# Moving a rare-case branch behind the last store, and reordering the first layer's chunks

## The chip, the core and the metric

The kernel runs on one core of a Trainium2 chip. The metric is device time in microseconds, as the median of several runs. A core has five engines that work side by side, each on its own list of instructions in order: TensorE (PE in the profile, its weight loads PEld), VectorE (DVE), ScalarE (ACT), GpSimd (POOL) and SyncE (SP). They wait for one another by semaphores. SP issues nearly all transfers from the chip's memory.

## The reference, cut to what matters

Four graph layers over 3327 nodes with 64 features and a dense, mostly zero adjacency matrix `adj` (3327 x 3327). After each layer the input is added and each row is normalised.

```python
def _L0_gnn_ref(features, adj, W):
    neigh = jnp.matmul(adj, features)
    deg = jnp.sum(adj, axis=1, keepdims=True) + 1.0
    return jnp.matmul(jnp.concatenate([features, neigh / deg], -1), W.T)

def _L1_gnn_ref(x, adj, weight, bias):      # hyperbolic log map of every pair of nodes
    w = adj / jnp.maximum(adj.sum(axis=1, keepdims=True), 1e-08)
    log_ij = _logmap(x[:, None, :], x[None, :, :], c)
    agg = jnp.einsum('ij,ijc->ic', w, log_ij)
    return _expmap(jnp.zeros_like(agg), agg @ weight + bias, c)

def _L2_gnn_ref(X, adj, W, b):              # mean over neighbours, relu, row norm
    ...

def _L3_gnn_ref(input, adj, weight, bias):
    support = input @ weight
    mask = (adj != 0).astype(support.dtype)
    rank = jnp.cumsum(mask, axis=1)         # which neighbour in the row is it?
    deg = rank[:, -1:]
    k = jnp.minimum(deg, float(MAX_NEIGH))
    pos = rank - (deg - k)
    w = mask * jnp.where(pos > 0, DECAY ** (k - pos), 0.0)
    return w @ support + bias

x = _layernorm(x + _L0_gnn_ref(x, adj, L0_gnn_W), axis=-1)
x = _layernorm(x + _L1_gnn_ref(x, adj, L1_gnn_weight, L1_gnn_bias), axis=-1)
x = _layernorm(x + _L2_gnn_ref(x, adj, L2_gnn_W, L2_gnn_b), axis=-1)
x = _layernorm(x + _L3_gnn_ref(x, adj, L3_gnn_weight, L3_gnn_bias), axis=-1)
```

## The kernel before

**Tiling.** The nodes are padded to 3328, that is 26 blocks of 128. The transposed adjacency is cut into four chunks of 832 target nodes (columns), and each chunk into 13 pairs of source blocks. One pair is a tile of 128 x 2 x 832 floats, 832 KB; `load_adj` brings it, by SP, into one of four rotating buffers (`adjp`) or into memory that is free for a while, such as `sums` or `uw`. Each layer reads the whole matrix again, chunk by chunk.

**Layer 0.** For each pair, `aggregate_pair` (L467) adds adjacency times features to the accumulator of the chunk in PSUM: 4 instructions, 8 records in the trace. The loop also does early work for layer 3, which needs every neighbour's rank. For three of the four chunks (all but `LATE_RANKS`, chunk 3) `Ranks.mask` makes a 0/1 mask of the pair on VectorE (L493). `count` turns masks into ranks: 12 matmuls of the mask with a triangle of ones (L539), a carry of the last row into the next mask on VectorE (`carry`, L525), and two copies to `rank` on ScalarE (L549). Masks that are made wait in a list, and `count(masked, places, left, ...)` works it down until `left` of them remain. Before, the chunks come in the order 0, 3, 1, 2 (`ORDER`), so the unranked chunk 3 stands second; the counts of chunk 0 are spread over chunks 0 and 3 (`L0_SPILL`), and in chunks 1 and 2 three masks stay behind (`L0_LAG`). They are counted after the last adjacency matmul.

Each chunk completes the sums of a group of blocks (`GROUPS`). `finish0` takes the group through `sums0` (transposes L582, division by the degree L590, sum of squares) and `features0` (the scaled features `xr` and `xu`, partly on GpSimd), in steps that are laid between the pairs of the next chunk. `transposes0` (L650) then writes the group into `ut` and `wt`, the two operands of layer 1. The last group goes through `sums0` at the end of the layer, and through `features0` and its transposes in layer 1's loop (`late`).

**The vote and the branch.** Layer 1 is computed for pairs of nodes. If all nodes have a large enough norm, a cubic in the scalar product is precise enough, which is `layer1_far`, the cubic path. If one has not, the general arm `layer1_near` must run. `sums0` notes the near nodes (L594) of each group; at the end of layer 0 VectorE, TensorE and VectorE reduce them to one number `n_near` (L775, L777, L778). Every engine loads it (L1466) and branches (L1468). For these inputs it is zero. Both arms go on with `layers_2_and_3`.

**Layer 1, cubic path.** For each of 104 items (chunk, source block) `far_v` (L835) multiplies `wt` and `ut` into one of three PSUM banks, VectorE forms the product p with the adjacency (L846), ScalarE squares (L859, L860, or L851), GpSimd or VectorE finishes the factor s (L861, L854), and `far_aggregate` (L866) adds it to the chunk's sum six items later. The first two pairs are loaded into `sums`, once the layer 0 sums there have been read; the loads of the others come after the branch.

**Order.** The instructions of each engine are placed by a scheduler; `issue_after` forces an instruction behind another on its engine, and is used all over to write the order down.

Of the kernel before, what the change touches and what calls it, by code (L numbers as in the profile page):

```python
# [41 lines left out]

ORDER2 = (2, 3, 1, 0)
# [35 lines left out]
L0_SPILL = 6  # L79
# [39 lines left out]
def four_gnn_layers_kernel(  # L119
# [148 lines left out]
    xu = nodes.tile([P, NB, D + 2], FP, name="xu")  # L268

# [305 lines left out]
    def sums0(c, bank):  # L575


        b0, b1_, nb = blocks_of(c)
        last = c == ORDER[-1]
# [25 lines left out]
    def features0(c, y, ss, work, aside=False):  # L605


        b0, b1_, nb = blocks_of(c)
# [31 lines left out]
    def finish0(c, bank):  # L640
        y, ss = yield from sums0(c, bank)
        yield from features0(c, y, ss, Work(blocks_of(c)[2]), True)

    def transposes0(c, place, behind=None, aside=False, k0=0, k1=GB):

        b0, _, nb = blocks_of(c)
# [11 lines left out]

    with ExitStack() as l0s:
        banks = Banks(l0s, "l0psum")  # L660
# [61 lines left out]
        first = GROUPS[3][0] * P  # L722
        load_xt(slice(first, NP))
        loaded = {jp: load_adj(ORDER[0], jp) for jp in (12, 11, 10)}
        load_xt(slice(0, first))
        masked, issued, counted, side = [], None, None, None
        for n, c in enumerate(ORDER):
# [4 lines left out]
            for jp in reversed(range(NB // 2)):  # L732
# [11 lines left out]
                left = (L0_SPILL - jp // 2 if ranks else jp // 2) if n < 2 else L0_LAG  # L744
# [3 lines left out]
                if side is not None and jp < NB // 2 - 1:  # L748
                    on_array = jp == NB // 2 - 2
                    if not step(side, (counted or issued) if on_array else mask if ranks else None):  # L750
                        side = None
                        transposes0(ORDER[n - 1], places.free(), counted or issued, True)
                        if n == NCH - 1:

                            nc.scalar.activation(nothing, wt[:, GROUPS[ORDER[n - 1]][0] * P].unsqueeze(1), AF.Tanh)
# [17 lines left out]
        count(masked, places, 0, counted)  # L773
        nearest = small.tile([P, 1], FP, name="nearest", tag="nearest")
        nc.vector.tensor_reduce(nearest, near, axis=AX.X, op=ALU.add)  # L775
        vote = banks.one(NCH % 2)
        nc.tensor.matmul(vote[0:1, 0:1], lhsT=nearest, rhs=ones, start=True, stop=True)  # L777
        nc.vector.tensor_copy(n_near, vote[0:1, 0:1])  # L778

    def adj_pairs(there):

        for c in ORDER:
            for jp in PAIRS:
                yield c, jp, there.pop(0) if there else load_adj(c, jp)
# [25 lines left out]
    def layer1_far(banks):  # L822
        with tc.tile_pool(name="l1w", bufs=1) as wp:
# [107 lines left out]
            work = Work(blocks_of(ORDER[-1])[2], banks.one(1))  # L931
            late = features0(ORDER[-1], *last_group, work)
            del work
            pairs = adj_pairs(first_pairs)
            waiting, last, side, total, summed, kept = [], None, None, NCH * NB, None, {}
            for start in range(0, total + L1_AHEAD, L1_GROUP):
                group = range(start, start + L1_GROUP)
                made = []
                for i in group:
                    if i < total:  # L940
# [5 lines left out]
                        v, v_issued = far_v(c, jb, summed)  # L946
# [3 lines left out]
                for i in group:  # L950
# [18 lines left out]

                    if late is None and i in (late_at, late_at + 2):  # L970
                        k0, k1 = (0, 4) if i == late_at else (4, GB)
                        transposes0(ORDER[-1], banks.one(1), v_issued, False, k0, k1)
# [23 lines left out]
            own = banks.pair()[:, 0, :]  # L996
# [6 lines left out]
    def layer1_near():  # L1003
        with ExitStack() as stack:
            all_of(features0(ORDER[-1], *last_group, Work(blocks_of(ORDER[-1])[2])))
            transposes0(ORDER[-1], Banks(stack, "l1b").pair())
# [184 lines left out]
    def begin2(banks, loading, loaded, behind):  # L1191
# [3 lines left out]
        rows = last_rows([(c, rank[:, c]) for c in ORDER2 if c != LATE_RANKS])  # L1195
        next(rows)
# [6 lines left out]
    def layers_2_and_3(banks, acc, done, rows, there):  # L1203


        with tc.tile_pool(name="l2m", bufs=10) as mp, tc.tile_pool(name="late", bufs=1) as late:
# [191 lines left out]
            for n, c in enumerate(ORDER2):  # L1398
# [9 lines left out]
                for i, jp in enumerate(order):  # L1408
# [17 lines left out]
                    if i == OWN2_AT:  # L1426
                        x2, based = prologue2(c, issued)
                        if n == 0:
                            step(rows, based)
                            all_of(rows)  # L1430
# [34 lines left out]

    some_near = nc.values_load(n_near[0:1, 0:1], min_val=0, max_val=NP)  # L1466

    with tc.If(some_near == 0) as cmp:  # L1468
        with ExitStack() as arm:
            banks = Banks(arm, "psum_far")  # L1470
            layers_2_and_3(banks, *layer1_far(banks))
    with cmp.Else():
        done = layer1_near()
        with ExitStack() as arm:
            banks = Banks(arm, "psum_near")
            with tc.tile_pool(name="l2a_near", bufs=8) as more:
                loading = load_ahead2(lambda k: more.tile([P, CH], FP, name="ahead", tag="ahead"))
                acc, rows = begin2(banks, loading, next(loading), None)
# [44 lines left out]
```

## Time and profile before

| | us |
|---|---|
| median of 3 runs | 524.47 |
| lowest and highest run | 524.07, 525.8 |
| span of the profiled execution, first to last instruction | 521.7 |
| layer 0, to the end of its last adjacency matmul | 143.25 |
| first matmul of layer 1 | 153.89 |
| first matmul of layer 2 | 350.4 |

The profile is one execution, and its span is the only time that is known of it; start and end of the program around the span, and the spread of the runs, make the rest of the median. The stretches of layers are read from the timeline. In the profile's rows a group of instructions has its line, engine, operation, output and inputs by name, shapes, and how often it comes; for DMA the bandwidth and the mean busy share of 16 engines are given, and for TensorE the clock that it was granted, as a share of full speed.

### The profile page before, as it was taken

To read this page: it belongs to the slowest core of one execution; us is meant where nothing else is said; L and a number is where in the kernel's file an instruction comes from. 1 tells how busy PE (TensorE), PEld (TensorE's weight loads), DVE (VectorE), ACT (ScalarE), POOL (GpSimd) and SP (SyncE) were. 2 spreads that over 40 slices of the span, in tenths; PEclk is the share of its full clock that TensorE was granted. 3 is DMA by queue.
4 is the path that set the end of the run, shared out by engine and by line. 5 is a ranking of instruction groups with operands and counts; after the bars stand their busy time and mean duration, and the time that the engine had idled before them with its cause. 6 is when DMAs were issued, how large, how long until landed. Compare 5 with 4: busy or idle time off the path is not lost.

```text
span 521.7 us, 8496 instructions
## 1 busy us (share of the span) xinstructions
PE 482.3 (92%) x3256; PEld 240.5 (46%) x3256; DVE 387.0 (74%) x703; ACT 336.7 (65%) x395; POOL 180.1 (35%) x150
## 2 busy tenths in 40 slices
PE   4999999999977999998999999999999999999994
PEld 3554344454432333443353344354465565556663
DVE  3565438989668987789879977988789876627744
ACT  1435545776868899978988896930277943337941
POOL 2001201112026778866886785700412012200000
PEclk9999999999978999999999999999999999999997
DMA  8999999989439688767776777579869979950002
GB/s 268 318 366 339 375 389 387 327 285 315 183 99 323 203 260 291 232 196 257 260 231 213 224 256 261 197 268 405 315 197 361 306 263 374 349 194 2 1 18 56
DMA packets 46211, 132.52 MB, mean 254 GB/s; under 512 B 6966, under 2 KB 7070, under 8 KB 46098
## 3 DMA queue, kind: packets, MB, share of 16 engines
q1 hardware_dynamic: 45634, 131.35, 72.7%
q0 software_dynamic: 384, 0.52, 0.3%
q8 instruction: 27, 0.44, 0.3%
q14 instruction: 22, 0.18, 0.1%
q10 hardware_dynamic: 144, 0.03, 0.0%
HBM read 130.86 MB, written 0.85 MB: 252 GB/s over the span
## 4 chain that ended last, share of the span: by engine, by line
PE 53%; DVE 24%; ACT 10%; DMA 6%; issue 3%; POOL 0%; ACTq 0%; DVEq 0%
PE one L467 16%; PE two L1333 10%; DVE p L846 8%; PE two L835 7%; DMA adj<-in_adjt_dram 6%; PE one L866 6%; PE two L539 5%; DVE mask L525 4%; PE two L467 4%; ACT s L859 3%; DVE s L854 3%; DVE mask L493 3%; ACT s L860 2%; ACT rank L549 2%; PE two L1238 1%
## 5 line engine op out<-in xcount | busy, mean ns | idle before, releaser
L861 POOL TENSOR_TENSOR s<-s,p 128x832 f32<-128x832 f32 x67 | 130.1, 1957 | 45.6 <-ACT s L860 32.3
L846 DVE SCALAR_TENSOR_TENSOR p<-two,adj 128x832 f32<-128x832 f32 x100 | 101.0, 1018 | 19.1 <-issue 14.4
L835 PE MATMUL two<-uw 64*128 64x416 f32 x416 | 91.6, 556 | 13.3 <-DVE s L854 7.2
L549 ACT ACTIVATE rank<-two,last_bias 128x832 uint8<-128x832 f32 x78 | 71.8, 952 | 45.0 <-PE two L539 23.0
L866 PE MATMUL one<-s,xu 128*64 128x416 f32 x416 | 85.2, 524 | 0.0
L467 PE MATMUL one<-adj,x0w 128*64 128x416 f32 x416 | 82.3, 522 | 2.7 <-ACT x0w L677 1.4
L859 ACT ACTIVATE s<-two,far_bias 128x832 f32<-128x832 f32 x67 | 63.6, 950 | 23.9 <-DVE p L846 21.6
L525 DVE SCALAR_TENSOR_TENSOR mask<-two,minus_last,mask 32x832 bf16<-32x832 f32 x48 | 52.5, 1093 | 29.5 <-PE two L539 26.0
L835 PEld LDWEIGHTS two<-uw 64*128 64x128 f32 x416 | 38.3, 192 | 66.7 <-PE one L866 22.6
L1333 PE MATMUL two<-bits,parts 128*64 128x416 bf16 x624 | 62.3, 339 | 0.0
L539 PE MATMUL two<-mask,tri 128*64 128x416 bf16 x416 | 52.9, 344 | 9.3 <-DVE mask L525 6.1
L493 DVE TENSOR_SCALAR mask<-adj 128x1664 bf16<-128x1664 f32 x48 | 51.5, 1073 | 13.4 <-DMA adj<-in_adjt_dram 12.6
L860 ACT ACTIVATE s<-s 128x832 f32<-128x832 f32 x67 | 60.1, 897 | 1.9
L467 PE MATMUL one<-adj,xr 128*64 128x416 f32 x264 | 57.0, 514 | 0.0
L1333 PEld LDWEIGHTS <-parts 128*64 128x64 bf16 x624 | 36.8, 110 | 24.2 <-issue 7.3
L866 PEld LDWEIGHTS one<-s,xu 128*64 128x64 f32 x416 | 25.9, 136 | 47.5 <-issue 46.6
L467 PEld LDWEIGHTS one<-adj,x0w 128*64 128x64 f32 x416 | 29.2, 138 | 35.0 <-issue 23.8
L539 PEld LDWEIGHTS <-tri 128*64 128x64 bf16 x416 | 25.6, 110 | 41.4 <-issue 23.6
L1303 ACT ACTIVATE bits<-rank 128x1664 uint16<-128x1664 uint8 x22 | 33.6, 1579 | 15.5 <-PE two L1333 14.6
L854 DVE SCALAR_TENSOR_TENSOR s<-two,p 128x832 f32<-128x832 f32 x37 | 37.6, 1016 | 2.9 <-ACT two L851 2.5
L851 ACT ACTIVATE two<-two,far_bias 128x832 f32<-128x832 f32 x37 | 34.0, 918 | 5.1 <-DVE p L846 4.9
L549 ACT ACTIVATE uw<-two,last_bias 128x832 uint8<-128x832 f32 x26 | 24.2, 950 | 12.5 <-DVE mask L525 6.4
(270 smaller groups left out, 471.1 us busy)
## 6 DMA issues: line engine op xcount, KB each, us to landing
adj<-in_adjt_dram SPq DMA_DIRECT2D x135, 832.0 KB, 5.4
uw<-in_adjt_dram SPq DMA_DIRECT2D x7, 832.0 KB, 7.4
a<-in_adjt_dram SPq DMA_DIRECT2D x8, 416.0 KB, 6.2
sums<-in_adjt_dram SPq DMA_DIRECT2D x2, 832.0 KB, 5.9
p<-in_adjt_dram SPq DMA_DIRECT2D x4, 416.0 KB, 4.7
s<-in_adjt_dram SPq DMA_DIRECT2D x4, 416.0 KB, 6.3
uw<-in_xt_dram SPq DMA_DIRECT2D x1, 640.0 KB, 11.1
out_dram<-o SPq DMA_DIRECT2D x3, 192.0 KB, 2.5
```

The lines of the kernel that those rows point to most:

```text
L467: issued = nc.tensor.matmul(acc[h * D : (h + 1) * D, 0:HC], lhsT=x[:, 2 * jp + k, 0:D], rhs=a[:, bass.ts(h, HC)], start=(first and k == 1) ...
L493: issued = nc.vector.tensor_scalar(mask, a2, 0.0, None, op0=ALU.not_equal)
L525: ranks.carried = nc.vector.scalar_tensor_tensor(halves(last), ranks.after[P - 32 : P, :, 0:HC], minus_last[P - 32 : P, :], halves(last), ...
L539: issued = nc.tensor.matmul(counts[k][rows, h, 0:HC], lhsT=lhsT[:, rows], rhs=mask[:, of, bass.ts(h, HC)], start=lhsT is tri, stop=(k == 1 ...
L549: ranks.made = nc.scalar.activation(halves(ranks.rank[:, 2 * jp + k, :]), counts[k][:, :, 0:HC], AF.Relu, bias=last_bias,)
L835: issued = nc.tensor.matmul(v[:, h, 0:HC], lhsT=wt[rows, bass.ts(jb, P)], rhs=ut[rows, bass.ds(c * CH + h * HC, HC)], start=True, stop=True,)
L846: issued = nc.vector.scalar_tensor_tensor(halves(p), v, 0.25 - 0.5 * FD, halves(a), op0=ALU.add, op1=ALU.mult)
L859: nc.scalar.activation(halves(s), v, AF.Square, bias=far_bias, scale=-2.0)
L860: nc.scalar.activation(s, s, AF.Copy, bias=FG)
L861: nc.gpsimd.tensor_mul(s, s, p)
L866: issued = nc.tensor.matmul(acc[h * D : (h + 1) * D, 0:HC], lhsT=xu[:, jb, 0:D], rhs=s[:, bass.ts(h, HC)], start=first, stop=last,)
L1333: issued = nc.tensor.matmul(acc3[c][h * D : (h + 1) * D, 0:HC], lhsT=parts[:, 2 * jp + b, bass.ts(part, D)], rhs=bits[:, b, bass.ts(h, HC) ...
```

## The change

It has three parts, which belong together.

1. **The branch goes to the end.** The cubic path is no longer an arm: it always runs, through all layers and the stores of the output. The vote's sum and matmul move from the end of layer 0 to the end of layer 1's loop (`vote`). After the last store every engine loads `n_near` and branches. If a node was near, the general arm computes layers 1 to 3 again and stores over the output. For that, layer 0's features `xr`, which layer 1 overwrites, are copied to memory (`kept_x1`, by GpSimd's queue) when the last group is done, and read back in the arm.
2. **One set of PSUM banks** (`psum_far`) serves layer 0 and all that follows. The scheduler can now mix the end of layer 0 with the start of layer 1: `ahead_of` holds layer 1's first products behind the last counts.
3. **Layer 0 in the order 0, 1, 2, 3** (`ORDER0`, `GROUPS0`), so that the unranked chunk comes last. The number of masks that may stay behind grows from 0 to 7 over the three ranked chunks and is worked down to 0 in chunk 3 (`L0_SPILL` is 8 now, which also adds two mask buffers). The last group is blocks 19 to 25; layer 1 takes the first chunk's pairs in natural order, so that these come last.

```diff
+ORDER0 = (0, 1, 2, 3)
+GROUPS0 = {0: (0, 6), 1: (6, 13), 2: (13, 19), 3: (19, 26)}
...
-L0_SPILL = 6
+L0_SPILL = 8
...
+    kept = ctx.enter_context(tc.tile_pool(name="kept", bufs=1, space=bass.MemoryType.DRAM))
+    kept_x1 = kept.tile([P, NB, D], FP, name="kept_x1")
...
+    far = ExitStack()
+    banks = Banks(far, "psum_far")
     with ExitStack() as l0s:
-        banks = Banks(l0s, "l0psum")
...
-        for n, c in enumerate(ORDER):
+        for n, c in enumerate(ORDER0):
...
-                left = (L0_SPILL - jp // 2 if ranks else jp // 2) if n < 2 else L0_LAG
+                done = n * (NB // 2) + NB // 2 - 1 - jp
+                left = L0_SPILL * jp // (NB // 2)
+                if ranks:
+                    left = min(done // 2, L0_LAG + (L0_SPILL - L0_LAG) * done // (3 * NB // 2))
                 counted = count(masked, places, left, issued)
...
-        count(masked, places, 0, counted)
+        counted = count(masked, places, 0, counted) or counted
+
+    def vote(bank, behind):
         nearest = small.tile([P, 1], FP, name="nearest", tag="nearest")
         nc.vector.tensor_reduce(nearest, near, axis=AX.X, op=ALU.add)
-        vote = banks.one(NCH % 2)
-        nc.tensor.matmul(vote[0:1, 0:1], lhsT=nearest, rhs=ones, start=True, stop=True)
-        nc.vector.tensor_copy(n_near, vote[0:1, 0:1])
+        issue_after(nc.tensor.matmul(bank, lhsT=nearest, rhs=ones, start=True, stop=True), behind)
+        nc.vector.tensor_copy(n_near, bank)
...
-            pairs = adj_pairs(first_pairs)
+            ahead_of = counted
+            pairs = adj_pairs(first_pairs, range(NB // 2))
...
-                        v, v_issued = far_v(c, jb, summed)
+                        v, v_issued = far_v(c, jb, summed or ahead_of)
...
+                    if late is None and i == late_at:
+                        nc.gpsimd.dma_start(out=kept_x1, in_=xr)
...
-            own = banks.pair()[:, 0, :]
+            own = banks.pair()
+            vote(own[0:1, 1, 0:1], summed)
+            own = own[:, 0, :]
...
     def layer1_near():
-        with ExitStack() as stack:
-            all_of(features0(ORDER[-1], *last_group, Work(blocks_of(ORDER[-1])[2])))
-            transposes0(ORDER[-1], Banks(stack, "l1b").pair())
+        nc.sync.dma_start(out=xr, in_=kept_x1)
...
+    with far:
+        layers_2_and_3(banks, *layer1_far(banks))
+
     some_near = nc.values_load(n_near[0:1, 0:1], min_val=0, max_val=NP)
 
-    with tc.If(some_near == 0) as cmp:
-        with ExitStack() as arm:
-            banks = Banks(arm, "psum_far")
-            layers_2_and_3(banks, *layer1_far(banks))
-    with cmp.Else():
+    with tc.If(some_near > 0):
         done = layer1_near()
         with ExitStack() as arm:
             banks = Banks(arm, "psum_near")
```

Elsewhere in layer 0, `ORDER` and `GROUPS` become `ORDER0` and `GROUPS0`. `begin2` leaves out, in the general arm, the last rows of the ranks, which are there by then. By the order of instructions, the small loads of `last_rows` on GpSimd's queue move from the branch up into layer 0.

## The prediction

> **What bounds the kernel now.** I read the page's busy line first, then the busy time in eight stretches cut at the chunks of layer 0 and at the layer borders, then the timeline round the branch, and last the queue entries at the program's end. Chunk borders are the first adjacency matmuls (L467) of each chunk, found by counting eight records to a pair of blocks.
>
> ```profile
> span 521.7 us, 8496 instructions
> PE 482.3 (92%) x3256; PEld 240.5 (46%) x3256; DVE 387.0 (74%) x703; ACT 336.7 (65%) x395; POOL 180.1 (35%) x150
> ...
> core 0: us, PE busy (x) PEld busy (x) DVE busy (x) ACT busy (x) POOL busy (x), PEclk, DMA share, GB/s
> 8.70:43.40 34.70, 32.24 (x223) 17.18 (x224) 23.03 (x42) 13.52 (x18) 0.64 (x4) 1.00 0.97 331
> 43.40:73.20 29.80, 28.18 (x204) 13.20 (x202) 11.31 (x29) 17.48 (x21) 3.60 (x5) 1.00 1.00 374
> 73.20:106.20 33.00, 31.14 (x230) 14.04 (x228) 27.42 (x46) 18.72 (x24) 4.80 (x4) 1.00 0.98 357
> 106.20:143.20 37.00, 34.66 (x276) 17.89 (x274) 30.72 (x46) 28.39 (x35) 5.19 (x4) 1.00 0.76 260
> 143.20:153.90 10.70, 6.83 (x61) 3.37 (x55) 7.47 (x18) 8.60 (x11) 0.30 (x1) 0.86 0.25 82
> 153.90:172.00 18.10, 14.83 (x56) 5.91 (x56) 13.82 (x28) 11.97 (x14) 13.28 (x12) 0.80 0.88 300
> 172.00:341.00 169.00, 160.18 (x827) 66.36 (x827) 144.87 (x227) 146.16 (x173) 127.13 (x66) 1.00 0.71 233
> 341.00:522.00 181.00, 171.48 (x1388) 99.90 (x1386) 125.88 (x259) 90.33 (x101) 21.75 (x20) 0.98 0.64 224
> ```
>
> TensorE sets the pace (over 92% busy) everywhere except in the fifth and sixth stretch, the 29 us round the branch, where nothing does: 6.83 of 10.70 us, 14.83 of 18.10, and DMA at a quarter. So an edit is worth there what it takes off the chain, and elsewhere what it takes off or puts on TensorE. The second stretch is chunk 3, the unranked one, second in the old order: DMA share 1.00, so transfers help to hold it.
>
> The timeline shows the chain at the branch:
>
> ```profile
> 141.66 1.59 PE L467 MATMUL one<-adj,x0w 128*64 128x416 f32 x8
> ...
> 147.42 1.09 DVE L525 SCALAR_TENSOR_TENSOR mask<-two,minus_last,mask 32x832 bf16<-32x832 f32 x1
> ...
> 152.74 0.15 DVE L778 CAST n_near<-one 1x1 int32<-1x1 f32 x1 [1.40 <-PE one L777]
> 153.89 5.06 PE L835 MATMUL two<-uw 64*128 64x416 f32 x16 [1.18 <-ACT rank L549]
> 155.85 1.02 DVE L846 SCALAR_TENSOR_TENSOR p<-two,sums 128x832 f32<-128x832 f32 x1 [2.96 <-PE two L835]
> ```
>
> Layer 0's last adjacency matmul ends at 143.25. Only then come the last four counts (12 matmuls of 1.05 us each, with a DVE carry of 1.09 us between one and the next), the last group's sums, the vote (L777, L778), 1.0 us of register load and branch, and the first layer 1 product at 153.89. The chain of waits agrees: from 143.25 on it runs through L525, L590, L591, L409, L414, L525 and three L549.
>
> **The change, part by part.** E is the end of layer 0's last adjacency matmul, 143.25 before.
>
> 1. Chunk order and counts. Before, 35 of the 39 counts lay ahead of E, after it all 39. In the old order the records of the count's first matmuls (L539 with tri, eight to a count) give 7 counts in the first stretch (56 records), 6 in the second (48), about 9 in the third (73 in the trace), 13 in the fourth up to E. The two ranked chunks of 13 pairs that run after each other thus took 33.0 us with about 9 counts and 37.0 with 13: 1.0 us more a count, which is the 1.05 of the row. That is my ruler. The new rule for what is left over (4 after chunk 0, 6 after chunk 1, 7 after chunk 2) gives 9, 11, 12 and 7 counts:
> chunk 0: 34.7 + 2 x 1.05 = 36.8;
> chunk 1: 33.0 + 2 x 1.05 = 35.1; chunk 2: 37.0 - 1.05 = 35.9;
> chunk 3: 29.8 + 1.05 = 30.8 if the transfers still hold it, 18.2 of L467 (13 x 1.40) + 7 x 1.05 + 1.5 of sums and transposes = 27.1 if TensorE alone does. It now comes after three chunks slower than the transfers, with all four buffers full, but one more 832 KB load (the first of layer 1, into `sums`) goes into its queue; I take 28.8.
> E = 8.7 + 36.8 + 35.1 + 35.9 + 28.8 = 145.3, 2 us later than before; between 142 (deferral also shortens the waits in chunks 1 and 2) and 148.
>
> 2. The junction. After E there are no counts, no vote and no branch ahead of layer 1. What DVE still has ahead of the first product p is the old chain up to L591, 143.25 to 147.39 (the one carry in it, at 144.34, ran beside the transposes, so its going saves nothing): p(0) starts at E + 4.15. In the changed kernel's order DVE then does p(0), L409, p(1), L414, the two near steps, p(2): 1.02 + 0.62 + 1.02 + 0.61 + 0.35 = 3.6, so p(2) at E + 7.8 = 153.1. Before, p(2) started at 158.10 (the second of three products merged at 157.08). Gain 5.0. From p(2) on the same rotation of three PSUM banks and the same instructions follow, so I carry 5.0 through to the end of layer 1.
> Transfers: before, four pairs were issued at once at 153.94 and landed after 4.3 to 11.5 us. In the new SP queue three of them stand ahead of layer 0's end, waiting only for buffers. The second load into `sums` waits for the last transposes, goes out at E + 2.2 and, at the 4.5 us of the same load before, lands at E + 6.7, before p(2). At the 7.3 us that the first one took, p(2) loses 1.7: kept for the range.
>
> 3. A rule against a row. The granted clock in stretches of 2 us:
>
> ```profile
> 152.00:154.00 2.00, 0.82 (x8) 0.23 (x4) 0.15 (x1) 1.73 (x2) 0.40 (x1) 0.50 0.00 0
> ...
> 162.00:164.00 2.00, 2.00 (x8) 1.04 (x6) 0.28 (x1) 1.39 (x2) 2.00 (x2) 0.50 1.02 311
> ```
>
> TensorE starts layer 1 at half clock and falls back to it at 162. The Trainium skill, TensorE: Matmul & The Clock Gate, section "Part 1: The HAM clock gate", says that the clock halves after an idle window of about 3.4 us. After the change the first gap is shorter (products 0 to 2 end near E + 3.3, product 3 can start at E + 6.2), so by the rule the clock stays up: 16 matmuls at 0.21 instead of 0.32 us, another 1.7 us gained. The row speaks for less: the drop at 162 followed a gap of only 1.83 us (158.94 to 160.77). I take 0 and keep 1.7 for the range.
>
> 4. POOL and SP queues. The memset and three `last_a` loads move up into layer 0; the three `last_more` copies of finished ranks are spread over it. One issue is 0.51 to 0.69 us (L563, L564). Each waits for ScalarE's last rank of its chunk, and POOL's xr or xu step and the copy to `twice`, which TensorE's transposes need, stand behind it. The leftover counts are done by about the seventh pair of the next chunk, the transposes come after the eleventh, so four pairs (10 us) cover it; without the cover TensorE would lose about a pair, 2.5 us. New is the copy of xr to DRAM, 832 KB, issued by POOL after the late group. No store of that size is in the trace; by L563 its issue is 0.5 to 0.7 us, and I double the upper end to 1.4. POOL runs about 3 us ahead of its user there (a product that started on POOL at 176.22 is needed near 181), so 0; 1.4 if not. Its 2 us of transfer lie in a layer with DMA share 0.71.
>
> 5. The vote goes to the end of layer 1, where TensorE runs without a gap: 0.2 us (L777, 0.19). Load of `n_near` on SP: 0.5 us (0.475 before) between layer 2 loads that are far ahead: 0.
>
> 6. The end. Every engine now loads `n_near` and branches after its last work.
>
> ```profile
> L1468 DVEq COMPARE_BRANCH  x1: 51/51/51, 517.6 to 517.6; - x1
> L1519 DVEq DRAIN  x2: 10/45/80, 520.8 to 521.2; - x2
> ```
>
> DVE's last branch, at 517.6, is followed by nothing for 3.2 us, beside the last store (landing 2.4 to 3.0). With the load ahead of it (0.544 on DVE) DVE arrives 0.5 later, just as the store ends: +0.5. The rule that speaks against this change is in the Trainium skill, Runtime: NRT & Kernel Launch, section "Instruction fetch mechanics": a taken branch to a target outside the fetched window stalls for a fetch. The changed program has two in sequence, over the general arm and then out of the empty other arm. The old end already pays one fetch; by the row the second target lies next to the first and costs its 0.05, by the rule at worst another 3.2. I take 0.5, up to 3.7.
>
> Below nothing for parts 4 to 6: a gain is excluded for 5 and 6, which only add instructions; in 4 the six issues leave POOL's junction, but its first product waited for ScalarE there (2.44 us idle), so no gain.
>
> Sum: -5.0 + 0.2 + 0.5 = -4.3 us on the profiled span of 521.7, to 517.4. The median of the runs, 524.47, is 2.8 above the span, and nothing in that difference is touched: 520.2.
>
> **The rivals.**
> A, a larger gain (0.18). Counts held back longer let masks and carries run without holding TensorE: half of the idle in chunks 1 and 2 goes (TensorE unbusy 1.9 and 2.3 us there, and more hidden in matmuls recorded at 1.6 instead of 1.4), E near 142, the clock stays up. -5.0 - 3.3 - 1.7 + 0.7 = -9.3: 515.2. For it: TensorE waits for L525 1.0 us at 125.97. Against: a carry waits for the count before it, however many are held.
> B, slower (0.15). Three ranked chunks in a row make the chain count, carry, count the bound, since DVE has mask 1.03 and carry 1.09 for each pair and group steps between. With a pair at p us in chunks 1 and 2, E = 8.7 + 36.8 + 26p + 29.8. The gain of 150.3 - E less the 0.7 is gone at p = 2.86; the fourth stretch ran at 37.0/13 = 2.85, the third at 2.54. At 3.0, E is 153.3 and the sum +3.7: 528.2. It is slower by more than can be told from 2.92 on. For it: the old pace with a full load of counts is at the edge. Against: 11 and 12 counts, not 13.
> C, it doesn't shorten the end (0.07): the second fetch is paid in full, -4.3 + 3.2 = -1.1: 523.4. For it: five engines show 2.4 to 3.5 us after their last branch. Against: the target is adjacent.
>
> **How the numbers follow.** The likeliest case (0.60) is 520.2; its own range, E between 142.5 and 147.5 with 1.7 either way for clock and landing, is 517 to 523.2, and about 0.05 of it lies within 0.3% (1.6 us, about what a measurement of this kernel can tell from no change). Faster 0.55 + 0.18 = 0.73; same 0.05 + 0.07 = 0.12; slower 0.15. For eight in ten the range goes from 513.5 (0.05 below) to 526 (0.12 above).
>
> **What would show it.** Right: E at 145, the first p about 4 us after E and no L777 between; p(2) near 153; layer 1's first product of the last chunk and everything to the last store shifted by one amount, about 5 us; DVE's last queue entry later after its last instruction by 0.5. Wrong: E beyond 149 with L539 waiting for L525 in chunks 1 and 2 (B); a gap above 4 us between the last store's issue and the end (C); transposes waiting for POOL in chunk 1 or 2 (part 4); p(2) waiting for the load into `sums`.

## The result: slower, by 1.6%

| | before | after | forecast |
|---|---|---|---|
| median of 4 runs each, us | 524.27 | 532.43 | 520.2 |
| lowest and highest run | 522.83, 525.8 | 530.0, 533.76 | range 513.5 to 526 |
| span of the profiled execution | 521.7 | 531.7 | 517.4 |
| E, end of layer 0's last adjacency matmul | 143.25 | 153.53 | 145.3 |
| E to product p of item 20 of layer 1 | 47.58 | 41.51 | 40.5 |
| start of layer 1's last sum to start of layer 2's first matmul | 3.85 | 6.57 | 4.05 |
| first to last adjacency matmul of layer 2 | 119.61 | 121.14 | 119.61 |
| last store's issue to the end | 3.68 | 5.23 | 4.2 |

The ratio of the runs is 1.0157, with a 95% interval of 1.0119 to 1.0194. The profiled execution of the changed kernel (533.74 us) is one of its longer ones, so the spans differ by 10.0 us where the medians differ by 8.2. Everything that the table leaves out, nearly all of layer 1 and of layers 2 and 3, runs as before.

The page of the changed kernel, and its busy time in stretches cut as before the change (here and in the prediction's table a chunk ends with its last adjacency matmul, to within 0.2 us): the four chunks of layer 0, the handover to layer 1 in two pieces, layer 1, the handover to layer 2, the rest, the end. After the stretch come its length, then the busy time of PE, PEld, DVE, ACT and POOL with instruction counts, the granted clock, the DMA share and GB/s.

```profile
span 531.7 us, 8503 instructions
...
PE 486.4 (91%) x3256; PEld 243.5 (46%) x3256; DVE 385.9 (73%) x703; ACT 337.0 (63%) x395; POOL 177.9 (33%) x151
...
8.90:49.40 40.50, 36.37 (x247) 19.20 (x248) 26.21 (x45) 16.09 (x21) 1.58 (x5) 0.96 0.92 292
49.40:84.50 35.10, 32.52 (x250) 15.58 (x247) 28.29 (x46) 24.70 (x30) 4.43 (x5) 1.00 0.92 314
84.50:122.80 38.30, 33.98 (x266) 17.11 (x265) 27.93 (x45) 25.06 (x31) 4.42 (x5) 1.00 0.94 330
122.80:153.50 30.70, 29.72 (x217) 14.23 (x213) 11.87 (x29) 20.32 (x25) 3.89 (x5) 1.00 0.98 349
153.50:162.50 9.00, 5.76 (x23) 2.49 (x21) 7.39 (x16) 3.29 (x5) 2.03 (x2) 0.81 0.71 259
162.50:176.10 13.60, 10.26 (x40) 3.81 (x40) 10.97 (x27) 9.37 (x11) 7.75 (x4) 0.75 0.37 124
176.10:345.10 169.00, 160.18 (x827) 66.28 (x827) 144.73 (x227) 146.17 (x173) 127.76 (x67) 1.00 0.72 238
345.10:361.00 15.90, 15.02 (x77) 8.47 (x76) 10.73 (x25) 3.33 (x5) 0.00 (x0) 0.79 0.89 323
```

In the long stretch of layer 1, a window of 169 us as before, TensorE has the same 827 records and the same 160.18 us as before, and from product p of item 20 to the last sum it takes 155.67 us (before: 155.69): nothing is wrong there. The loss lies in four places. The first chunk takes 40.5 us, with a clock of 0.96. The third takes 38.3 and the last 30.7, with transfers at a share of 0.98 in the last. The handover from layer 1 to layer 2 ran at a clock of 0.79; before, TensorE went through it at full clock. And the end is 1.55 us longer. The handover to layer 1 is shorter, as it was meant to be.

The start of layer 0, from the timeline:

```profile
4.96 1.68 POOL L570 DMA_DIRECT2D last_a<-in_adjt_dram  x3
...
13.56 1.03 DVE L500 TENSOR_SCALAR mask<-adj 128x1664 bf16<-128x1664 f32 x1 [3.88 <-DMA adj<-in_adjt_dram]
14.50 0.61 DVE L686 COPY xr<-two 128x126 f32<-128x126 f32 x2
14.84 0.89 PE L546 MATMUL two<-mask,tri 128*64 128x416 bf16 x8 [2.87 <-DVE xr L686]
```

The third mask in the kernel before, and the transfers of the changed one between 8 and 10 us (queue: packets, MB, share of 16 engines):

```profile
11.21 1.03 DVE L493 TENSOR_SCALAR mask<-adj 128x1664 bf16<-128x1664 f32 x1 [1.64 <-DMA adj<-in_adjt_dram]
```
```profile
q1 hardware_dynamic: 175, 0.57, 80.3%
q0 software_dynamic: 47, 0.15, 22.0%
```

GpSimd issues its three last_a loads at 5 us. They run on a queue of their own, q0, beside the adjacency on q1, and the mask of the third adjacency pair can only start at 13.56 (before: 11.21). VectorE makes xr after it, TensorE needs that bank for its first count and waits 2.87 us; from 15.8 to 19.2 it then runs at half clock.

The handover to layer 1:

```profile
157.43 1.02 DVE L848 SCALAR_TENSOR_TENSOR p<-two,sums 128x832 f32<-128x832 f32 x1
...
159.48 1.76 PE L837 MATMUL two<-uw 64*128 64x416 f32 x4 [1.98 <-ACT s L861]
...
160.44 1.94 POOL L863 TENSOR_TENSOR s<-s,p 128x832 f32<-128x832 f32 x1 [6.84 <-DVE ss_last L421]
160.45 1.94 DVE L601 SCALAR_TENSOR_TENSOR near_nodes<-ss_last,real 128x7 f32<-128x7 f32 x1
162.43 0.18 DVE L790 TENSOR_REDUCE nearest<-near_nodes 128x1 f32<-128x26 f32 x1
162.53 1.95 DVE L848 SCALAR_TENSOR_TENSOR p<-two,sums 128x832 f32<-128x832 f32 x2
```

The near step of the last group in the kernel before (shortest, median and longest ns, first and last start):

```profile
L594 DVE SCALAR_TENSOR_TENSOR near_nodes<-ss_last,real x1: 166/166/166, 151.0 to 151.0; 128x7 f32<-128x7 f32 x1
```

p(0) starts at E + 3.9 and p(2) at E + 9.0. TensorE's first gap lasts 1.98 us; 1.6 us into it, at 159.1, the clock falls to half and stays there for 10.2 us. Look at the near step on VectorE: 128 x 7 elements took 1.94 us, as long as GpSimd's product that started 0.01 us before it. The same instruction took 0.17 us in the kernel before, where GpSimd was idle.

The handover to layer 2:

```profile
351.15 0.19 PE L791 MATMUL two<-ones,nearest 128*1 128x1 f32 x2
...
352.04 0.13 DVE L792 CAST n_near<-two 1x1 int32<-1x1 f32 x1
...
352.23 1.95 PE L891 MATMUL two<-w1r,uw 64*128 64x64 f32 x14 [0.89 <-DVE n_near L792]
354.10 3.25 PE L905 MATMUL two<-wl,sums 128*128 128x66 f32 x14
...
357.28 5.99 PE L474 MATMUL two<-uw,xr 128*64 128x416 f32 x24
```

The same three groups in the kernel before:

```profile
346.96 1.77 PE L889 MATMUL two<-w1r,uw 64*128 64x64 f32 x14
...
348.66 1.78 PE L903 MATMUL two<-wl,sums 128*128 128x66 f32 x14
...
350.37 4.41 PE L467 MATMUL two<-uw,xr 128*64 128x416 f32 x24
```

The vote's matmul is done at 351.34. The next one, L891, writes to the other bank of the pair that the vote is in, one tile for the program, and waits 0.89 us until VectorE has copied the vote out, which had two other instructions ahead of it. 14 matmuls of L905 then take 3.25 us (before: 1.78), as the clock fell to half at 353.7 and stayed there for 6.8 us.

The end, by the queue entries of SyncE and VectorE (how often, shortest, median and longest ns, first and last start):

```profile
L1478 SPq EVENT_SEMAPHORE  x8: 17/17/17, 527.4 to 530.0; - x8
...
L1478 DVEq COMPARE_BRANCH  x1: 72/72/72, 526.6 to 526.6; - x1
...
L1478 DVEq EVENT_SEMAPHORE  x1: 21/21/21, 529.9 to 529.9; - x1
```
```profile
L1525 SPq EVENT_SEMAPHORE  x14: 17/28/28, 530.1 to 531.6; - x14
```

The last store, before and after (KB, us from issue to landing):

```profile
out_dram<-o SPq DMA_DIRECT2D x1, 128.0 KB, 2.6
```
```profile
out_dram<-o SPq DMA_DIRECT2D x1, 128.0 KB, 3.4
```

The 1.55 us have two parts. The last store, issued at 526.47, landed at 529.91, after 3.44 us, where it took 2.62 before: 0.82. From there to the end it is 1.79 us, before 1.06: 0.73. SyncE waits for the last store inside the branch (L1478), until 530.0. Only then comes the program's own closing row of waits (L1525), the first twelve of which took from 530.1 to 530.8. In the kernel before, nine of those twelve waits were over while the store was still under way.

### The profile page after: what moved, and what is told of

It reads as the page before. It is cut to its first block, busy times and chain, and to the rows that moved or that the text cites. A ratio compares the mean times of both kernels' runs of the same rounds, so it can differ in the third digit from the quotient of the medians.

```text
span 531.7 us, 8503 instructions
## 1 busy us (share of the span) xinstructions
PE 486.4 (91%) x3256; PEld 243.5 (46%) x3256; DVE 385.9 (73%) x703; ACT 337.0 (63%) x395; POOL 177.9 (33%) x151
## 4 chain that ended last, share of the span: by engine, by line
PE 52%; DVE 22%; DMA 10%; ACT 8%; issue 3%; POOL 1%; ACTq 0%; POOLq 0%; DVEq 0%
PE one L474 17%; DMA adj<-in_adjt_dram 10%; PE two L1340 10%; DVE p L848 8%; PE two L546 6%; PE two L837 5%; PE one L868 4%; DVE s L856 4%; PE two L474 4%; ACT s L861 3%; ACT s L862 3%; DVE mask L532 2%; DVE mask L500 2%; PE two L905 1%; PE two L1245 1%
## 5 line engine op out<-in xcount | busy, mean ns | idle before, releaser
L837 PE MATMUL two<-uw 64*128 64x416 f32 x416 | 93.9, 553 | 15.4 <-ACT s L861 7.7
L474 PE MATMUL one<-adj,x0w 128*64 128x416 f32 x416 | 83.8, 531 | 1.6 <-DMA adj<-in_adjt_dram 1.0
L500 DVE TENSOR_SCALAR mask<-adj 128x1664 bf16<-128x1664 f32 x48 | 50.4, 1051 | 23.0 <-DMA adj<-in_adjt_dram 22.5
L546 PE MATMUL two<-mask,tri 128*64 128x416 bf16 x416 | 52.5, 342 | 11.3 <-DVE mask L532 6.6
L474 PE MATMUL one<-adj,xr 128*64 128x416 f32 x264 | 58.1, 514 | 0.2 <-DMA adj<-in_adjt_dram 0.2
```

The lines of the kernel that those rows point to most:

```text
L474: issued = nc.tensor.matmul(acc[h * D : (h + 1) * D, 0:HC], lhsT=x[:, 2 * jp + k, 0:D], rhs=a[:, bass.ts(h, HC)], start=(first and k == 1) ...
L500: issued = nc.vector.tensor_scalar(mask, a2, 0.0, None, op0=ALU.not_equal)
L546: issued = nc.tensor.matmul(counts[k][rows, h, 0:HC], lhsT=lhsT[:, rows], rhs=mask[:, of, bass.ts(h, HC)], start=lhsT is tri, stop=(k == 1 ...
L837: issued = nc.tensor.matmul(v[:, h, 0:HC], lhsT=wt[rows, bass.ts(jb, P)], rhs=ut[rows, bass.ds(c * CH + h * HC, HC)], start=True, stop=True,)
```

## The experiments

Each kernel was timed beside the kernel before. The ratio is to that, with its 95% interval; 1% is 5.2 us. Times in a trace are of one execution each.

**The two halves alone.** **old_order** is the changed kernel without its third part (its diff follows), **order_only** the kernel before with nothing but it.

```diff
-ORDER0 = (0, 1, 2, 3)
-GROUPS0 = {0: (0, 6), 1: (6, 13), 2: (13, 19), 3: (19, 26)}
+ORDER0 = ORDER
+GROUPS0 = GROUPS
-L0_SPILL = 8
+L0_SPILL = 6
...
-                left = L0_SPILL * jp // (NB // 2)
...
+                left = (L0_SPILL - jp // 2 if ranks else jp // 2) if n < 2 else L0_LAG
...
-            pairs = adj_pairs(first_pairs, range(NB // 2))
+            pairs = adj_pairs(first_pairs)
```

order_only takes over the lines of the change's diff on ORDER0, GROUPS0, L0_SPILL, left and adj_pairs, and none of the others.

> The changed kernel without its third part: chunk order 0, 3, 1, 2, groups, spill of 6 and the old rule for masks left over; the branch stays at the end, PSUM in one set. Theory S + V (start-up loads and vote cost 3.5 and 4.3 us whatever the order, the end 1.5): layer 0 ends about 3 us later than before, the handover to layer 1 gains about 1.5 to 2 us (branch and vote gone, the four counts still there), in all 532 us, as with the new order. Rival O (the new order and the new counts are the loss in layer 0): layer 0 ends where it ended before, 143.3, and the whole takes 528.5 us.

> The kernel before, with only the third part of the change: chunk order 0, 1, 2, 3, the new groups, a spill of 8 and the new rule for masks left over; branch and vote stay at the end of layer 0. Theory S (the start-up loss comes from GpSimd's loads, which stay behind the branch here): first chunk 36.8, then 35.1, 38.3 and 30.7, layer 0's adjacency ends at 149.6, and with no counts behind it the second product p(2) starts about 160, 2 us later than before: 526.3 us. Rival O (order and counts make the start-up loss): it ends at 153, p(2) near 163.5, 529.8 us.

Measured: old_order 1.0117 (1.0088 to 1.0146), order_only 1.0032 (1.0012 to 1.0052). Together that is 1.0149, against 1.0157 for the whole change: within the intervals the halves add up, and each of them loses. In old_order E came at 147.34, 4.1 us later than before, with the third mask at 13.33 and half clock from 15.7: the loss at the start shows in the old order too. (before_warm below, with the layer 0 of the kernel before, has E at 145.12, so the 4.1 is not exact.) In order_only the chunks took 37.7, 34.5, 38.0 and 30.5 us, E came at 149.41 and item 20 at 192.42, 1.6 us later than before: 6.2 us lost ahead of E, 4.6 gained behind it. order_only went as theory S had it. In old_order only the start did: the gain of 1.5 to 2 us at the handover to layer 1 did not come (E to item 20 took 48.04 us, before 47.58), and the vote cost 1.1 us instead of 4.3, as shown below.

**The loads at the start.** In **rows_late** GpSimd's memset of last_more and the loads and copies behind it must follow its last product of layer 1.

```diff
-        nc.gpsimd.memset(more, 200.0)
+        issued = [nc.gpsimd.memset(more, 200.0)]
...
+        if behind is not None:
+            for one in issued:
+                issue_after(one, behind)
```

> The changed kernel, with only GpSimd's memset of last_more, the three last_a loads and the three copies to last_more held back behind layer 1's last GpSimd product; the change had let them move up into the start of layer 0. Theory S (the last_a loads beside the first adjacency loads made the third pair land at 13.5 instead of 11.2 us; TensorE waited 2.87 us and then ran at half clock): the first chunk is about 3.5 us shorter, and the whole 528.9 us, 0.9% over the kernel before. Rival R (the counts that now start one pair earlier cause the wait): no difference, 532.4.

Measured: 1.0054 (1.002 to 1.0088), so some 5 us of the loss are gone. In its timeline, and in its transfers between 8 and 10 us:

```profile
10.85 1.03 DVE L500 TENSOR_SCALAR mask<-adj 128x1664 bf16<-128x1664 f32 x1 [1.32 <-DMA adj<-in_adjt_dram]
11.80 0.61 DVE L690 COPY xr<-two 128x126 f32<-128x126 f32 x2
12.13 0.89 PE L546 MATMUL two<-mask,tri 128*64 128x416 bf16 x8 [0.63 <-DVE xr L690]
```
```profile
q1 hardware_dynamic: 245, 0.84, 108.8%
```

The third mask starts at 10.85, TensorE waits 0.63 instead of 2.87 us, and E is 149.44, 4.1 us earlier; 3.0 of these are there at the end of the first chunk (46.46, after the change 49.49). Over all kernels: with the loads at the start the third mask came at 12.59 to 13.56 us (three kernels), without them at 10.6 to 11.3 (eleven, the kernel before among them). The adjacency's queue moved 0.84 MB in these 2 us, and 0.57 with the loads beside it. So the three loads of 84.5 KB each hold back the adjacency. The counts, which rival R blamed, were unchanged here. The size is less sure than the cause: with the same layer 0 and without the early loads, E came at 148.06 to 153.09 in six executions (rows_late and five kernels below, mean 149.9), with them at 153.53 and 154.70, and by the medians the loads cost 1.03% (here) and 0.38% (v_mid against vmid_rows, next).

**The vote.** In **v_mid** the vote stands at item 26 of layer 1, in a bank that is idle there; **vmid_rows** has this and the late loads.

```diff
+VOTE_AT = 26
...
+                    if i == VOTE_AT:
+                        vote(banks.one(1)[0:1, 0:1], v_issued)
...
-            vote(own[0:1, 1, 0:1], summed)
```

> The changed kernel, with only the vote moved: from the end of layer 1 (in the bank pair of the last own products) to item 26 of layer 1's loop, in a bank that is idle there. Theory V (the vote in the handover from layer 1 to layer 2 makes TensorE wait 0.89 us for VectorE's copy of n_near, and the half clock from 353.7 to 360.5 follows from that wait): the handover is as short as before the change, 4.3 us less, about 528.1 us, 0.7% over the kernel before. Rival W (the half clock there has nothing to do with the vote): 0.9 us less, about 531.5, and the half clock stays.

> The changed kernel with both undone: GpSimd's first part of last_rows held behind layer 1, and the vote at item 26 of layer 1. Theory S + V, that the two costs are separate and add up (4.1 us of start-up, 1.1 us of waiting at the handover to layer 2, and a half clock there in some executions): span 522.9, 1.1 less than with the loads held back alone; ratio to the kernel before 1.000 to 1.003. Rival (the vote costs the same wherever it stands): 1.0054 as with the loads held back alone.

Measured: v_mid 1.0087 (1.0059 to 1.0115), vmid_rows 1.0049 (1.0027 to 1.007), 526.35 us. The handover is back at 3.85 us in both. The changed kernel's 6.57 was not the vote's fixed price, though: rows_late has the same vote, and this handover:

```profile
348.35 1.77 PE L895 MATMUL two<-w1r,uw 64*128 64x64 f32 x14 [0.89 <-DVE n_near L796]
350.05 1.78 PE L909 MATMUL two<-wl,sums 128*128 128x66 f32 x14
351.75 1.62 PE L474 MATMUL two<-uw,xr 128*64 128x416 f32 x8
```

The wait of 0.89 us is there, the half clock is not: 4.92 us from sum to matmul. old_order reads 4.93, and so do keep4 and lag3, which follow below. So the wait and the matmul itself cost 1.1 us each time, and the half clock, another 3.2 us, followed it in one of five profiled executions. So theory V and rival W were both half right. No run has the vote at the old place in a bank of its own, so bank and place are not told apart. The step from rows_late to vmid_rows is 0.05% by the medians, where the traces show 1.1 us (0.2%); the intervals of the two cover that. vmid_rows missed its 1.000 to 1.003: 1.0049.

**The near step.** In **near_late** the last group's near step and the sum over near move to the vote at item 26. In **near_early** these two stand at item 20, and the vote's matmul and copy at item 28. Both start from vmid_rows. The diff is near_early's; in near_late all of it is in `vote`.

```diff
+NEAR_AT, VOTE_AT = 20, 28
...
+                    if i == NEAR_AT:
+                        nearest = near_sum(p_issued)
+                    if i == VOTE_AT:
+                        vote(nearest, banks.one(1)[0:1, 0:1], v_issued)
...
+        if not last:
+            near_step(ss, b0, b1_)
```

> As vmid_rows, and in addition the last group's near step (128 x 7) and the sum over near move out of the handover from layer 0 to layer 1, to the vote at item 26. Theory N (the near step took 1.94 instead of 0.17 us because it ran beside GpSimd's first product, and p(2) waited for it): p(2) comes 1.9 to 2.1 us earlier relative to layer 0's end, and 1.2 to 2 us are left at item 20 of layer 1; ratio about 0.997 to 1.000. Rival M (another VectorE instruction takes the long slot beside GpSimd, or TensorE's half clock sets product 4): p(2) moves, item 20 doesn't, ratio as vmid_rows.

> As near_late, with the near step and the sum over near at item 20 of layer 1, and only the vote's matmul and copy at item 28: VectorE's sum is ready long before TensorE comes to the vote. Theory G (of the 2.2 us that p(2) gained in near_late 1.4 were given back at item 26, because TensorE waited there for VectorE's sum): item 100 of layer 1 comes at layer 0's end + 185.7 to 186.0 instead of 187.1, and the ratio to the kernel before is 0.2 to 0.3% under that of near_late. Rival H (whatever VectorE does in the loop for the vote costs the same, wherever its parts stand): 187.1, and the same ratio.

Measured: near_late 1.0068 (1.0041 to 1.0096), near_early 1.0031 (1.0011 to 1.0051). In near_late p(2) came at E + 6.8 instead of 9.0, and item 20 also 2.2 us earlier, at E + 39.5. So the near step did hold the handover. But item 100 came at E + 187.1, against 187.9 in vmid_rows: 1.4 us were given back at the vote. The ratio is outside theory N's 0.997 to 1.000, and its interval covers that of vmid_rows in great part.

```profile
202.36 0.65 DVE L587 SCALAR_TENSOR_TENSOR near_nodes<-ss_last,real 128x7 f32<-128x7 f32 x1
...
203.87 0.16 DVE L802 TENSOR_REDUCE nearest<-near_nodes 128x1 f32<-128x26 f32 x1
...
204.08 0.19 PE L803 MATMUL one<-ones,nearest 128*1 128x1 f32 x2 [0.52 <-DVE nearest L802]
```

TensorE, with its instructions in order, waited for a sum that VectorE had made only just before. near_early, with the sum eight items ahead of the vote, has item 100 at E + 186.4: half of the 1.4 is back, less than theory G had. Its lower ratio is more than the trace explains (0.8 us would be 0.15%), so I don't read the ratio as that step alone.

**The counts.** **keep4** is rows_late with four masks left until after E, as before the change; **lag3** is rows_late with never more than three masks left over.

```diff
 keep4
-                left = L0_SPILL * jp // (NB // 2)
+                left = max(4, L0_SPILL * jp // (NB // 2))
 lag3
-                left = L0_SPILL * jp // (NB // 2)
+                left = min(L0_LAG, jp)
                 if ranks:
-                    left = min(done // 2, L0_LAG + (L0_SPILL - L0_LAG) * done // (3 * NB // 2))
+                    left = min(done // 2, L0_LAG)
```

> The changed kernel with the loads held back (rows_late), and in addition four masks left over through the last chunk, so that four of the 39 counts run behind layer 0's last adjacency matmul, as before the change. Theory Z (moving the four counts ahead of it is paid in full, 1.05 us of TensorE each): layer 0 ends 4.2 us earlier than in rows_late, at 145.2, and item 20 of layer 1 comes 0 to 4 us later than there, since count, carry and count now follow one another with nothing between: ratio 1.005 to 1.013. Rival D (transfers hold the last chunk, so counts in it are free): layer 0 ends where it did, 149.4, and the whole is 4 us or more slower than rows_late.

> The changed kernel with the loads held back (rows_late) and chunk order 0, 1, 2, 3, but with never more than three masks left over: the counts of a chunk are done in it, 10, 13, 13 and 3 instead of 9, 11, 12 and 7. Theory T (the last chunk is held by its transfers at 29.5 to 30 us, so counts left for it cost little, and counts taken out of it bring little): layer 0 ends 3 to 4 us later than in rows_late, about 153, ratio 1.011 to 1.013. Rival U (TensorE holds the last chunk, counts cost 1.05 us wherever they stand): it ends at 149.4 as in rows_late, ratio 1.005.

Measured: keep4 1.0176 (1.0142 to 1.0209), lag3 1.0119 (1.0084 to 1.0153). The last chunk of each, in the order rows_late, keep4, lag3. By the records of their matmuls these have 7.8, 5.3 and 3.0 counts in it; in keep4 the scheduler had drawn part of the four counts ahead of E again:

```profile
118.29:149.44 31.15, 29.78 (x215) 14.17 (x211) 11.89 (x29) 20.25 (x25) 3.46 (x4) 1.00 0.96 344
```
```profile
118.58:148.25 29.67, 27.00 (x184) 12.33 (x181) 9.70 (x27) 14.01 (x19) 3.46 (x4) 1.00 0.96 344
```
```profile
123.61:153.52 29.91, 24.90 (x155) 10.25 (x153) 7.51 (x25) 9.95 (x15) 3.45 (x4) 1.00 0.98 360
```

Read the length against TensorE's busy time behind it: in lag3 TensorE has 4.9 us less to do than in rows_late, and the chunk is only 1.2 us shorter. What holds it is the transfers: TensorE waits for the adjacency there for 4.4 us in all, in keep4 for 1.9, in rows_late for 0.8, at a DMA share of 0.96 to 0.98. So theory T holds for lag3's last chunk (and E came at 153.52, as said, though part of that is a first chunk of 40.8 us, and E moves by as much without an edit). keep4's chunk is 1.5 us shorter for 2.5 counts less, where theory Z asks 2.6, while E to item 20 grew from 41.69 to 46.34. That is nearer to rival D, and so is the ratio: 1.2% over rows_late, some 6 us, and above theory Z's 1.013. Counts left for the unranked chunk cost 0.3 to 0.6 us each there instead of 1.05, and having them ahead of E is worth it. What the order does not give is a chunk under 29.7 us.

**The clock in the handover to layer 1.** **warm** is near_early with 40 idle matmuls where TensorE waits there, **before_warm** the kernel before with 32.

```diff
+WARM = {2: 16, 3: 14, 5: 10}
...
+                        for _ in range(WARM.get(i, 0)):
+                            beat = nc.tensor.matmul(
+                                spare[:, 416:512], lhsT=ident, rhs=ident[:, 0:96], start=True, stop=True
+                            )
```

> As near_early, with 40 idle matmuls (ident by 96 columns, into columns of a bank that nothing reads) behind layer 1's products 2, 3 and 5, where TensorE waits for the bank of the next product. Theory K (TensorE's two waits of 2 and 1 us in the handover let the clock drop to half for 7 to 10 us, and this holds back products 4 to 8): the clock stays up there, item 20 comes 1.5 to 3 us earlier relative to layer 0's end (36.5 to 38 instead of 39.5), ratio 0.3 to 0.6% under near_early. Rival L (VectorE, ScalarE and GpSimd set the pace there, or the idle matmuls stand in the way): no gain or a loss of up to 3 us.

> The kernel before, unchanged but for 32 idle matmuls of the same kind behind products 2, 3 and 5 of layer 1. Theory K: its half clock from 161.1 to 164.5 goes, at most 1.7 us less, ratio 0.997 to 1.000; the drop at 150.9 comes earlier than these matmuls and stays. Rival L: 1.000 to 1.006.

Measured: warm 1.0043 (1.0021 to 1.0065), before_warm 1.0054 (1.0029 to 1.0079). From warm's timeline:

```profile
152.42 3.81 PE L968 MATMUL one<-ident 128*128 128x96 f32 x32
156.16 0.97 PE L852 MATMUL two<-uw 64*128 64x416 f32 x4
157.06 3.37 PE L968 MATMUL one<-ident 128*128 128x96 f32 x28
160.35 1.67 PE L852 MATMUL two<-uw 64*128 64x416 f32 x8
```

The clock did stay up (0.994 over the whole run, with no half clock until the end), but 16 idle matmuls last 3.8 us in a gap of 2, and item 20 came at E + 41.4 instead of 39.5. I had made them too many. In before_warm too the drop at 161 was gone, and item 20 came at E + 50.3 instead of 47.6. So rival L's second half held in both: the idle matmuls stood in the way. What the half clock there costs by itself stays open.

**The end.** **no_arm** is near_late without load, branch and general arm; it leaves out the case of a near node.

```diff
-    some_near = nc.values_load(n_near[0:1, 0:1], min_val=0, max_val=NP)
-    with tc.If(some_near > 0):
...
```

> As near_late, without the load of n_near, the branch and the general arm: the case of a near node is left out, so it computes the outputs only where no node is near. Theory E (the extra end is SyncE's second row of twelve waits behind the last store and the late landing of that store): the time from the last store's issue to the end falls from about 4.9 to 3.7 us or less, 1.2 us less than near_late. Rival F (the end is set by the store, whatever follows): no difference that can be told.

Measured: 1.0006 (0.9982 to 1.0029), 0.6% under near_late. From the last store's issue to the end it takes 2.96 us, against 5.50. With the branch behind the stores that stretch was 4.8 to 5.5 us (ten kernels), with the branch at the end of layer 0 it was 3.7 to 4.1 (three), with no branch 3.0. Cut at the store's landing, the part behind it was 1.8 to 1.9 us in the ten, and 1.0 to 1.2 in the other four: that is the second row of waits, 0.6 to 0.9 us, as theory E had it. The part ahead of it, the store itself, took 3.0 to 3.7 us in the ten, 2.6 to 3.1 in the three and 2.0 with no branch. So of the 2.5 us that no_arm gained, where theory E had 1.2, 0.8 are the row and 1.7 the store. Why the store lands later behind a branch is not shown; in near_late six packets of instructions (two queues, 0.06 MB) ran beside the last stores and after them, in no_arm one (0.01 MB).

No version beat the kernel before. The best of those that compute everything are near_early, 1.0031, and order_only, 1.0032.

## Why the prediction was wrong

The sum was -4.3 us and the traces give +10.0. The 14.3 us between are, by the steps of the prediction: E 8.2, the junction 1.0, the vote 4.1, the end 1.0.

**Step 4 (GpSimd's and SyncE's queues, 0 us)** failed. It priced the issue on GpSimd and asked who stands behind it on that queue. It never asked what the moved loads would meet: the first adjacency pairs, for which all engines wait at the start. By rows_late that is 3.0 us by the end of the first chunk, half clock included, and 4.1 at E.

**Step 1 (E)** failed in the remaining 4.1: rows_late has chunks of 37.8, 35.3, 36.5 and 31.2 us, where 36.8, 35.1, 35.9 and 28.8 were forecast. The ruler of one microsecond to a count was good in the ranked chunks. The last chunk was mis-sized: I had allowed four full buffers to lift it under the transfers' 29.8, and lag3 and keep4 show that it stays there. TensorE's own sum, 27.1, was too small as well: it was busy for 29.78 of the 31.15 us in rows_late. 0.96 us of that is layer 1's first product, which the shared bank set let in ahead of E (at 144.48); what it does to the chunk's length was not tested. The third chunk moves between 35.5 and 38.3 us from one execution to the next, with no edit near it, and the first one between 37.7 and 42.7 even without the early loads. In two of the long first chunks, near_late's and near_early's, TensorE waits once for 2.2 to 2.4 us at the weights w1h, in rows_late 0.6, and near_early's has 6.8 us of half clock; why stays open. So the shares of steps 4 and 1 in the 8.2 us hold to some 2 us only.

The prediction's opening put DMA at a quarter all round the branch; that is the fifth stretch of its table, the sixth has 0.88.

**Step 2 (junction)** was right in kind and nearly in size. p(0) came at E + 3.9 (forecast 4.15), nothing of vote or branch between. p(2) came at E + 9.0, not 7.8, since the near step, counted in 0.35 us for two, took 1.94 beside GpSimd. That it was this is shown by near_late. The forecast that layer 1 carries one shift through held, from item 20 to its last sum.

**Step 3 (clock, 0)** was right, and for its reason. The rule of the Trainium skill that was weighed there (TensorE: Matmul & The Clock Gate, section "Part 1: The HAM clock gate") would have kept the clock up in a gap of 1.98 us; it was at half for 10.2 us from 159.1, as long as in the two drops before the change together. That the two agree so closely is in part chance: in other kernels it was 6.8 us at this place.

**Step 5 (vote, 0.2)** failed: it priced the matmul and not the next matmul, which writes to the vote's pair of banks and waits for a VectorE copy. That is 1.1 us, and in this execution 3.2 more of half clock.

**Step 6 (end, 0.5)** was too small, 1.55 us, and had the wrong engine. VectorE's load and branch end at 526.7 and its next entry comes at 529.87: the 3.2 us of the prediction's row, once and not twice, and over 0.04 us ahead of the store's landing. The late one is SyncE, which waits for its queues twice (0.73 us), behind a store that itself landed 0.82 us later.

**The rivals.** A's sign did not come: E was never near 142 in the new order. C's did, more than 4 us from the last store's issue to the end (5.23), but VectorE shows no second 3.2 us. B had the right side by the wrong way: its sign came (E at 153.5, and TensorE waited 2.3 and 2.4 us in chunks 1 and 2 for the carries), but the pace of chunks 1 and 2 was (35.1 + 38.3) / 26 = 2.82 us a pair, under its break-even of 2.86. Of the two halves, the branch's move is worth 1.3 us at the junction (E to item 20 in rows_late 41.69, in order_only 43.01) and pays 1.1 at the vote and about 1.2 at the end, before any start-up loss. The new order gains 4.6 and pays 6.2.

## What to carry to other kernels

When an instruction may move up, look at what it will run beside, not only at what it leaves: a small load beside the first large ones can cost more than the branch it was freed from. Where one tiny result is handed from VectorE to TensorE and back, count the next matmul in the same banks as waiting for it, or move it away into a bank of its own and let the producer run several steps ahead. Work deferred into a stretch fills only what its bound leaves over; a chunk held by its transfers does not get shorter because its buffers are full at the start.

## What had not been expected of the hardware

- A VectorE step of 128 x 7 elements with both inputs in SBUF took 1.94 us instead of 0.17 when GpSimd's product had started 0.01 us before it (1.94 to 1.95 us in the changed kernel, v_mid, rows_late and vmid_rows; 0.65 us at item 26 in near_late, where the product had run for 1.3 us). The Trainium skill, SBUF — State Buffer, section "SBUF: two separate sides", says that such a VectorE step and a GpSimd step that reads SBUF lock each other out; the traces agree: in all five the step ended 0.02 us behind GpSimd's product.
- Half clock came in pieces of 3.4 us or a multiple (3.4, 6.8, 10.2), but for the last piece at the program's end, and once it began only 1.0 us into a wait of 1.98 us (near_late, 157.2). One and the same wait of 0.89 us was followed by it in one profiled execution and not in four others. Here the clock of a stretch could not be told from its gaps alone.
- The same kernel's runs spread by 1.3% (the kernel before in one set: 520.74 to 527.73), so one trace shows where time goes, and the medians with their intervals show what a change is worth.
